# A graph layer on one core: gathers tied to the edge factors, tasks dealt anew, and four tensor operations moved from VectorE to GpSimd

## The chip, the core and the metric

The kernel runs on one core of a Trainium2 chip. The core has five engines with an instruction queue each: TensorE (PE, whose weight loads the profile lists apart as PEld), VectorE (DVE), ScalarE (ACT), GpSimd (POOL) and SyncE (SP), and 16 DMA engines. Each engine takes its instructions in the order in which the program gives them; between engines only semaphores order things. The metric is the device time of one execution in microseconds (us), lower is better.

## What is computed

A layer of a graph network with 1250 nodes of 512 features and 40000 edges, sorted by their target `dst`. Cut to what matters:

```python
# x: (1250, 512); per edge: source, target, a 3-vector n, a distance r
s_j   = silu(x[src][:, 384:] @ W1 + b1) @ W3 + b3            # a table of 1250 rows
basis = sqrt(2/R) * sin(k*pi*r/R) / r * cutoff(r) @ W2 + b2   # k = 1..20
s1, s2, s3 = split(s_j * basis)
msg = [ v_j * s1 + s3 * n ,  s2 ]                             # 384 + 128 features
x   = x + segment_sum(msg, dst)                               # first sum over edges
row = update(x)                                               # per node: U, V, Wu1, Wu2
x   = x + segment_sum(row[src], dst)                          # second sum over edges
out = layernorm(x_in + x)
```

## The kernel before

**Front.** A table with one row of 640 floats per node (128 + 128 factors and the scaled vector part) is computed in ten blocks and written to DRAM. Edge data are turned by TensorE so that edges lie on the partitions.

**Main loop.** The 40000 edges are cut into chunks of 512, four chunks to a group (20 groups). A step `t` takes tile `i` of each of the four chunks of group `g`: four tiles of 128 edges. `NT` is 80 steps, four per group, and the groups go in pairs, so that the work repeats every eight steps. In each step:

- `gather` (POOL, L693) issues four indirect DMAs that fetch the source rows into `rows_t`, of which there are four buffers, and then two memsets of a tile `idle` that nobody reads (L704). It is called two steps ahead (`ahead = 2`).
- `edge_factors` (PE, L792) multiplies the basis with `W2` into `eb`. There is one `eb` tile in PSUM: the factors of step t+1 can be written only when `messages(t)` has read those of step t.
- `messages` (DVE, L804 and L807) multiplies rows and factors. Between its two products `make_pair` (DVE, L821) marks target and source for the links.
- `add_messages` (PE, L838, L845) sums the messages of step t-1 into the window of their group, `count_links` (PE, L863) counts how often each source occurs for each target, and `mark_sources` (ACT, L777, L780) makes the one-hots for that.

**Per group.** `make_turns` (DVE L713, L719, L723; ACT L725 the sine) makes the sines' arguments for two groups at once, `make_basis` (DVE, L734) the basis of a group, `turn_basis` (PE L743, copied by ACT L748) transposes it for `edge_factors`; `make_hot` (L752) and `make_spread` (L765, two halves) on DVE make the matrices that PE sums with. `close_group` copies the sums out of PSUM and splits the counts on ACT; `add_counts` finishes them on DVE.

**Per block of 128 nodes (two groups).** A chain over some ten steps (`sum_block`, `take_block`, `turn_nodes`, `times_u`, `times_uv`, `lengths`, `root`, `hidden`, `curve`, `factors`, `scale_row`, `end_row`) computes the node's second message, which is split in three bf16 parts: `part_row` and `less_part` (ACT L1048, DVE L1050, L1053). `begin_out` already multiplies counts with finished parts for some of the output blocks in PSUM.

**End.** After the loop the last block's chain runs, `add_out` does the remaining products, POOL adds up the rests (L1103, L1105), and `end_out` and `norm_out` normalize and store.

**What sets the order.** Nothing is scheduled automatically. The steps' tasks are put in lists by hand (`first`, `early`, `late`, `dve`), and the loop runs these lists at fixed places of a step. The order on each engine is the order of these calls. The loop's core:

```python
        for t in range(max(*early, *late, *dve) + 1):
            if t + ahead < NT:
                gather(t + ahead)
            if t < NT:
                messages(t)
            run(first, t)
            ...
```

Of the kernel before, what the change touches and what calls it, by code (L numbers as in the profile page):

```python
# [20 lines left out]
P = 128  # L21
# [516 lines left out]
def windowed(tc, sh):  # L538
# [55 lines left out]
    resid = tc.dram_tile([NP, width], F32, name="resid")  # L594
    counts = sh.counts
# [10 lines left out]
    with tc.tile_pool(name="msg", bufs=4) as pool, tc.tile_pool(  # L606
# [15 lines left out]
        quarter = pool.tile([P, 1], F32, name="quarter", bufs=1)  # L622
        fade = pool.tile([P, NE], F32, name="fade", bufs=1)
# [8 lines left out]
        def ratios():  # L632
            nc.vector.tensor_scalar(ratio, every, 1.0 / R_CUT, 1.0, op0=ALU.mult, op1=ALU.min)
            nc.vector.memset(quarter, 0.25 * TWO_PI)

# [50 lines left out]
        idle = pool.tile([P, 2, 160], F32, name="idle", bufs=1)  # L686

        def gather(t):
            g, i = batches[t]
            rows_t = pool.tile([P, CPG, V + 2 * C], F32, name="rows_t", bufs=ROWS)  # L690
            for j in tiles(g, i):
                n = lanes(g, i, j)
                nc.gpsimd.indirect_dma_start(  # L693
                    out=rows_t[:n, j, :],
                    out_offset=None,
                    in_=sh.table1,
                    in_offset=bass.IndirectOffsetOnAxis(
                        ap=sh.src_i[:n, g, i * CPG + j : i * CPG + j + 1], axis=0
                    ),
                )  # L700
            rows_of[t] = rows_t

            for k in range(2):
                nc.gpsimd.memset(idle[:, k, :], 0.0)  # L704


        def make_turns(g, n, part):
# [3 lines left out]
            if part == 0:  # L711
                share = ratio[:, g * EPG : (g + n) * EPG].rearrange("p (g t) -> p g t", t=EPG)
                nc.vector.tensor_mul(  # L713
# [10 lines left out]
            if part == 3 or part == 2 and g > 0:  # L724
                nc.scalar.activation(args, args, AF.Sin, scale=TWO_PI)  # L725
# [7 lines left out]
        def make_basis(g):  # L733
            nc.vector.tensor_mul(  # L734
# [35 lines left out]

        def mark_sources(t):

            g, i = batches[t]
            one = pool.tile([P, CPG, P], F16, name="one", bufs=3)
            for j in tiles(g, i):
                e = g * EPG + i * CPG + j
                nc.scalar.activation(one[:, j, :], number[:, :P], AF.Abs, bias=low[:, e : e + 1])  # L777
            for j in tiles(g, i):
                e = g * EPG + i * CPG + j
                nc.scalar.activation(  # L780
                    one[:, j, :], one[:, j, :], AF.Relu,
                    scale=less[:, e : e + 1], bias=worth[:, e : e + 1],
                )
            onehots[t] = one


        def edge_factors(t):
            g, i = batches[t]
            eb = ps_work.tile([P, CPG, BANK], F32, name="eb")
            for j in tiles(g, i):  # L790
                rows = slice(j * FEAT, j * FEAT + N_RBF + 1)
                nc.tensor.matmul(  # L792
# [3 lines left out]
            ebs[t] = eb  # L796

        def messages(t):
# [6 lines left out]
            make_pair(t)  # L805
            for js, n, m in runs(g, i):
# [64 lines left out]
        def close_group(g):  # L871
# [5 lines left out]
            else:  # L877
                if g + 2 < NGR:
                    assert rows == P
                    sums[g + 2] = pool.tile([P, width], F32, name="sums_1", bufs=2)  # L880
                    nc.scalar.copy(sums[g + 2][P - WIN :, :], agg[P - WIN :, :])
# [3 lines left out]
                rows = min(rows, KEPT)  # L885
                nc.scalar.copy(sums[g][:rows, :], agg[:rows, :])
# [7 lines left out]
            boths[g] = both  # L894

        def add_counts(g):
            both = boths.pop(g)
# [3 lines left out]
            del adjs[g]  # L901

# [19 lines left out]
        def sum_block(b):  # L922
            blk = work()
            for k in range(2):
                nc.tensor.matmul(
                    blk, sh.sel[:, k, :], sums.pop(2 * b + k), start=(k == 0), stop=(k == 1)
                )
            blks[b] = blk
# [116 lines left out]
        def part_row(b, k):  # L1045
# [3 lines left out]
            else:  # L1049
                nc.vector.tensor_sub(table2(b, 2), x1s.pop(b), table2(b, 1))  # L1050

        def less_part(b):
            nc.vector.tensor_sub(x1s[b], x1s[b], table2(b, 0))  # L1053
# [27 lines left out]
        def load_x(first):  # L1081
# [5 lines left out]
            for b in range(first, first + n):  # L1087
                if b in (0, NB - 1):
                    load_nodes(nc.scalar, sh, to, b, b + 1, cols, first)
            inner = [b for b in range(first, first + n) if b not in (0, NB - 1)]  # L1090
            load_nodes(nc.scalar, sh, to, inner[0], inner[-1] + 1, cols, first)
            for k in range(n):
                kept[first + k] = to[:, k, :]

        def load_rest(first):
            n = min(5, NB - first)
            to = five_rows("msg", 2)
            nc.scalar.dma_start(to[:, :n, :], rows_from(resid, first, n))
# [20 lines left out]
        def begin_out(b, a, last, kept):  # L1119
            if a == 0:  # L1120
                accs[b] = ps_sum.tile([P, BANK], F32, name="begun")
            products(accs[b], b, a, a + 1, a == 0, last and not kept)
            if last and not kept:
                partial[b] = pool.tile([P, width], F32, name=f"begun_{b}", bufs=1)
                nc.scalar.copy(partial[b], accs.pop(b))
# [9 lines left out]
        def end_out(b):  # L1135
# [8 lines left out]
            nc.vector.tensor_scalar(scale[:, 0:1], moments[:, 1:2], EPS, None, op0=ALU.add)  # L1144
            nc.scalar.activation(scale[:, 0:1], scale[:, 0:1], AF.Sqrt)
            ending[b] = row, moments, scale

        def norm_out(b):
            row, moments, scale = ending.pop(b)
            nc.vector.reciprocal(scale[:, 0:1], scale[:, 0:1])  # L1150
            nc.vector.tensor_scalar(
                scale[:, 1:2], moments[:, 0:1], scale[:, 0:1], -1.0, op0=ALU.mult, op1=ALU.mult
            )
# [11 lines left out]
        first, early, late, dve = {}, {}, {}, {}  # L1165

        def at(when, step, fn, *args):
            when.setdefault(step, []).append((fn, args))

        def pair_turns(g, part, t):  # L1170
            n = min(2, NGR - g)
            if n > 0:
                at(dve, t, make_turns, g, n, part)

        for k in range(3):
            pair_turns(1, k, 0)
        for g in range(NGR):
            at(early, last_step[g] + 1, close_group, g)
            at(dve, last_step[g] + 1, add_counts, g)
        for t, (g, i) in enumerate(batches):  # L1180
            if t + 1 < NT:
                at(early, t, mark_sources, t + 1)
            if g + 1 < NGR:
                if g % 2:
                    if i == 0:
                        at(dve, t, make_hot, g + 1)
                        at(early, t, turn_basis, g + 1)
                    elif i == 1:
                        at(dve, t, make_spread, g + 1, 0)
                        pair_turns(g + 2, 0, t)  # L1190
                    elif i == 2:
                        at(dve, t, make_spread, g + 1, 1)
                else:
                    if i == 1:
                        at(dve, t, make_hot, g + 1)
                    elif i == 2:
                        at(dve, t, make_basis, g + 1)
                        at(dve, t, make_spread, g + 1, 0)
                    elif i == 3:
                        at(first, t, turn_basis, g + 1)  # L1200
                        at(dve, t, make_spread, g + 1, 1)
                        if g + 2 < NGR:
                            at(dve, t, make_basis, g + 2)
        begin, begins, ends = 0, [], {}
        for b in range(NB):
            begin = max(last_step[2 * b + 1] + 1, begin + 8)
            at(late, begin, sum_block, b)
            at(dve, begin + 1, take_block, b)
            at(dve, begin + 2, keep_rest, b)
            at(early, begin + 2, turn_nodes, b)  # L1210
            at(early, begin + 3, times_u, b)
            at(late, begin + 3, times_uv, b)
            at(late, begin + 4, lengths, b)
            at(first, begin + 5, root, b)
            at(early, begin + 5, hidden, b)
            at(first, begin + 6, curve, b)
            at(early, begin + 6, factors, b)
            at(dve, begin + 7, scale_row, b)
            at(first, begin + 8, end_row, b)
            begins.append(begin)  # L1220
            ends[b] = end = begin + 8
            steps = (1, 4, 5, 6) if end < NT else (0, 0, 0, 0)
            for when, step, fn, *args in (
                (first, steps[0], part_row, b, 0), (dve, steps[1], less_part, b),
                (late, steps[2], part_row, b, 1), (dve, steps[3], part_row, b, 2),
            ):
                at(when if end < NT else dve, end + step, fn, *args)

        for g in range(3, NGR, 2):
            pair_turns(g, 1, last_step[g - 2])  # L1230
            pair_turns(g, 2, last_step[g - 2] + 1)
# [3 lines left out]
        for c, of in zip(range(4, NB), ((1,), (3,), (0, 4), (5,), (6,), (2,))):  # L1235
            for k, b in enumerate(of):
                n = begun[b] = c - 1 if k == len(of) - 1 else c - 2
                begin, long = begins[c - 1] + 4 * k, 8 // len(of)
                for a in range(n):
                    t = begin + a * (long - 1) // (n - 1)  # L1240
                    at(early, t, begin_out, b, a, a == n - 1, c == NB - 1)
# [3 lines left out]
        for first_b in range(0, NB, 5):  # L1245
            at(dve, free, load_x, first_b)
# [454 lines left out]
```

## Time and profile before

| | |
|---|---|
| median of 17 runs | 555.43 us (551.39 to 559.36) |
| the profiled execution | 555.12 us; span in the profile 553.2 us, so 1.9 us lie around it |
| granted TensorE clock, mean | 0.921 |
| PE | 445.0 us busy, 80% |
| DVE | 431.8 us busy, 78% |
| ACT | 359.2 us busy, 65% |
| POOL | 392.1 us busy, 71% |
| the gathers' DMA queue (q0) | 104.86 MB, 63.5% of 16 engines |
| first gather starts, last gather ends | 34.99 us, 473.65 us |
| last message of the loop ends | 489.85 us |

A row of the groups gives line, engine, operation, output and inputs, the count, the busy time and the mean of one in ns, and the idle time of the engine just before with what ended it ("issue": nothing that the profile shows). A row of the timeline gives start, length, engine, line and operation.

### The profile page before, as it was taken

To read this page: it belongs to the slowest core of one execution; us is meant where nothing else is said; L and a number is where in the kernel's file an instruction comes from. 1 tells how busy PE (TensorE), PEld (TensorE's weight loads), DVE (VectorE), ACT (ScalarE), POOL (GpSimd) and SP (SyncE) were. 2 spreads that over 40 slices of the span, in tenths; PEclk is the share of its full clock that TensorE was granted. 3 is DMA by queue.
4 is the path that set the end of the run, shared out by engine and by line. 5 is a ranking of instruction groups with operands and counts; after the bars stand their busy time and mean duration, and the time that the engine had idled before them with its cause. 6 is when DMAs were issued, how large, how long until landed. Compare 5 with 4: busy or idle time off the path is not lost.

```text
span 553.2 us, 11300 instructions
## 1 busy us (share of the span) xinstructions
PE 445.0 (80%) x4318; PEld 236.8 (43%) x4318; DVE 431.8 (78%) x594; ACT 359.2 (65%) x897; POOL 392.1 (71%) x524
## 2 busy tenths in 40 slices
PE   3945667678878878887887888989798788999993
PEld 2522323344444444444444445445444444445441
DVE  6587877978798898697999889789789789551682
ACT  1436473774887779379588687867957958723341
POOL 7338888887888788787888888888888888200960
PEclk9965888968898998797999999899899899999998
DMA  8557888878888877787788788778878778309131
GB/s 250 203 172 222 235 234 238 266 230 239 253 249 233 242 241 228 238 263 229 231 257 241 227 253 250 230 232 256 243 233 258 228 238 239 91 0 329 66 133 61
DMA packets 35179, 121.19 MB, mean 219 GB/s; under 512 B 6365, under 2 KB 7912, under 8 KB 35116
## 3 DMA queue, kind: packets, MB, share of 16 engines
q0 software_dynamic: 26016, 104.86, 63.5%
q1 hardware_dynamic: 5124, 9.69, 4.8%
q10 hardware_dynamic: 3976, 5.82, 3.1%
q8 instruction: 36, 0.59, 0.4%
q14 instruction: 27, 0.22, 0.1%
HBM read 111.89 MB, written 8.46 MB: 218 GB/s over the span
## 4 chain that ended last, share of the span: by engine, by line
PE 35%; DVE 23%; POOL 16%; ACT 9%; issue 8%; DMA 8%; DVEq 0%; POOLq 0%; ACTq 0%
POOL rows_t L693 13%; DVE msg L807 10%; PE agg L838 6%; PE eb L792 5%; DVE msg L804 5%; PE agg L845 5%; DMA wu_sb<-in_L_gnn_Wu_dram 4%; PE work L986 4%; DVE pair L821 3%; DMA rows_t<-table,src_i 3%; PE adj L1110 2%; PE agg L1110 2%; PE eb L1110 2%; ACT one L780 2%; PE begun L1110 2%
## 5 line engine op out<-in xcount | busy, mean ns | idle before, releaser
L693 POOL DMA_INDIRECT rows_t<-table,src_i x313 | 321.0, 1025 | 97.9 <-issue 81.2
L807 DVE TENSOR_TENSOR msg<-rows_t,eb 128x1536 f32<-128x1536 f32 (+1 forms) x81 | 137.0, 1692 | 0.0
L780 ACT ACTIVATE one<-one,weight,src_f 128x128 f16<-128x128 f16 x313 | 128.2, 481 | 0.2 <-DVE magic L674 0.2
L804 DVE TENSOR_TENSOR msg<-rows_t,eb 128x1024 f32<-128x1024 f32 (+1 forms) x81 | 95.4, 1178 | 40.5 <-PE eb L792 30.7
L792 PE MATMUL eb<-w_sb,basis_t 21*128 21x384 f32 x626 | 77.5, 551 | 61.2 <-DVE msg L807 60.2
L777 ACT ACTIVATE one<-number,low 128x128 f16<-128x128 f16 x313 | 99.4, 389 | 2.9 <-PE adj L863 1.5
L838 PE MATMUL agg<-msg,hot 128*32 128x512 f32 x626 | 97.9, 683 | 0.0
L845 PEld LDWEIGHTS agg<-msg,spread 128*32 128x32 f32 x1878 | 63.0, 122 | 59.3 <-issue 58.8
L845 PE MATMUL agg<-msg,spread 128*32 128x128 f32 x1878 | 77.1, 298 | 0.0
L792 PEld LDWEIGHTS eb<-w_sb,basis_t 21*128 21x128 f32 x626 | 27.2, 188 | 86.0 <-issue 58.4
L1110 PEld LDWEIGHTS <-counts 128*128 128x128 f16 x300 | 29.1, 98 | 27.6 <-issue 2.4
L1103 POOL TENSOR_TENSOR msg<-msg,rows_t 128x512 f32<-128x512 f32 (+1 forms) x10 | 13.9, 1399 | 37.2 <-PE eb L1110 37.2
L898 DVE SCALAR_TENSOR_TENSOR both<-both,adj 128x400 f16<-128x400 f16 (+1 forms) x20 | 11.3, 567 | 35.8 <-ACT both L893 29.2
L821 DVE TENSOR_TENSOR pair<-number,column 128x640 f16<-128x640 f16 (+1 forms) x81 | 38.2, 473 | 0.0
L863 PE MATMUL adj<-pair,one 128*128 128x160 f16 x313 | 38.2, 248 | 0.0
L765 DVE TENSOR_TENSOR spread<-hot,attr 128x768 f32<-128x768 f32 x40 | 37.9, 950 | 0.0
L704 POOL MEMSET idle<- 128x160 f32 x160 | 34.5, 254 | 0.0
L986 PE MATMUL work<-ident,square 128*128 128x128 f32 x60 | 14.0, 381 | 22.7 <-ACT basis_t L748 22.7
L1110 PE MATMUL begun<-store,counts 128*128 128x512 bf16 x117 | 31.5, 379 | 0.0
L1043 ACT COPY x<-work 128x128 f32<-128x128 f32 x10 | 2.7, 265 | 42.0 <-PE work L986 42.0
L863 PEld LDWEIGHTS <-one 128*128 128x128 f16 x313 | 21.3, 102 | 18.0 <-issue 15.4
L838 PEld LDWEIGHTS agg<-msg,hot 128*32 128x32 f32 x626 | 13.2, 112 | 34.0 <-issue 24.6
(171 smaller groups left out, 577.3 us busy)
## 6 DMA issues: line engine op xcount, KB each, us to landing
rows_t<-table,src_i POOLq DMA_INDIRECT x313
resid<-x SPq DMA_DIRECT2D x10, 256.0 KB
msg<-resid ACTq DMA_DIRECT2D x2, 1280.0 KB
rows_t<-in_x_dram ACTq DMA_DIRECT2D x2, 1024.0 KB
out_dram<-msg SPq DMA_DIRECT2D x8, 256.0 KB
table<-msg SPq DMA_DIRECT2D x6, 320.0 KB
store<-in_x_dram POOLq DMA_DIRECT2D x2, 768.0 KB
table<-rows_t SPq DMA_DIRECT2D x4, 320.0 KB
```

Of the source, the lines that this page charges most:

```text
L693: nc.gpsimd.indirect_dma_start(out=rows_t[:n, j, :], out_offset=None, in_=sh.table1, in_offset=bass.IndirectOffsetOnAxis(ap=sh.src_i[:n, g ...
L765: nc.vector.tensor_mul(spread[g][:, at], hots[g][:, at, None, :].to_broadcast([P, n, 3, WIN]), sh.attr[:, g, at, :, None].to_broadcast([P, ...
L777: nc.scalar.activation(one[:, j, :], number[:, :P], AF.Abs, bias=low[:, e : e + 1])
L780: nc.scalar.activation(one[:, j, :], one[:, j, :], AF.Relu, scale=less[:, e : e + 1], bias=worth[:, e : e + 1],)
L792: nc.tensor.matmul(eb[:, j, :V], turned[g][rows, i, :], sh.w2_sb[rows, :], start=True, stop=True,)
L804: nc.vector.tensor_mul(msg[:m, js, V:], rows_t[:m, js, V:], eb[:m, js, C:V])
L807: nc.vector.tensor_mul(msg[:m, js, :V].rearrange("p t (k c) -> p t k c", k=3), rows_t[:m, js, :V].rearrange("p t (k c) -> p t k c", k=3), ...
L821: nc.vector.tensor_tensor(pair[:m, js, :].rearrange("p t (l h) -> p t l h", h=2), number[:m, : PARTS * WIN].rearrange("p (l h) -> p l h", ...
L838: nc.tensor.matmul(agg[j * WIN : (j + 1) * WIN, :], hots[g][:m, i * CPG + j, :], msg[:m, j, :width], start=(i == 0), stop=False, skip_grou ...
L845: nc.tensor.matmul(agg[j * WIN : (j + 1) * WIN, c * C : (c + 1) * C], spread[g][:m, i * CPG + j, c, :], msg[:m, j, width:], start=False, s ...
L863: nc.tensor.matmul(to[:, :, at : at + WIN], one[:m, j, :], pair[:m, j, :].rearrange("e (p n) -> e p n", n=WIN), start=(i == 0 and j == js[ ...
L1110: nc.tensor.matmul(acc, counts[:, a, b * P : (b + 1) * P], table2(a, k), start=(start and a == first and k == 0), stop=(stop and a == end ...
```

## The change

Gathers: the two memsets go; a gather is called three steps ahead instead of two, after `edge_factors(t + 1)`, and its first DMA waits for the last matmul of these factors. Four operations move from DVE to POOL: `make_basis` (but for group 0), the product of `make_turns` (but for the first groups), and for all blocks but the last the two subtractions `less_part` and the third `part_row`; they stand in a new list `pool_` that runs right after the gather of a step. `make_pair` comes after both products of `messages`. The tasks of a group and of a block are dealt to other steps and carry a rank within a step; `close_group` copies the rows that the next odd group needs last, and `add_counts` is split in two. In the front all table rows come before the turning of weights and vectors. Other output blocks are begun in the loop (0 to 7, 120 matmuls instead of 111 there), each is stored to DRAM and loaded at the end, and the end's loads are issued by SP instead of ACT. In `end_out` and `norm_out` two small DVE operations become ACT operations.

```diff
-        def gather(t):
+        def gather(t, behind=None):
             ...
-                nc.gpsimd.indirect_dma_start(
+                got = nc.gpsimd.indirect_dma_start(
             ...
+                if behind is not None and j == 0:
+                    tc.add_manual_dep(
+                        got.ins, behind.ins.name, sync,
+                        reason="so that rows come while PE is ahead of DVE",
+                    )
             rows_of[t] = rows_t
-
-            for k in range(2):
-                nc.gpsimd.memset(idle[:, k, :], 0.0)
...
             if part == 0:
+                engine = nc.gpsimd if g > 1 else nc.vector
                 ...
-                nc.vector.tensor_mul(
+                engine.tensor_mul(
...
-        def make_basis(g):
-            nc.vector.tensor_mul(
+        def make_basis(g, engine):
+            engine.tensor_mul(
...
                 nc.vector.tensor_mul(msg[:m, js, V:], rows_t[:m, js, V:], eb[:m, js, C:V])
-            make_pair(t)
-            for js, n, m in runs(g, i):
...
-                nc.vector.tensor_sub(table2(b, 2), x1s.pop(b), table2(b, 1))
+                engine = nc.gpsimd if b < NB - 1 else nc.vector
+                engine.tensor_sub(table2(b, 2), x1s.pop(b), table2(b, 1))
 
         def less_part(b):
-            nc.vector.tensor_sub(x1s[b], x1s[b], table2(b, 0))
+            engine = nc.gpsimd if b < NB - 1 else nc.vector
+            engine.tensor_sub(x1s[b], x1s[b], table2(b, 0))
...
+        for g in range(1, NGR, 2):
+            base, n = 4 * g - 4, min(2, NGR - g)
+            at(pool_ if g > 1 else dve, max(0, base - 2), 4, make_turns, g, n, 0)
+            at(dve, max(0, base - 1), 6, make_turns, g, n, 1)
+            at(dve, base, 6, make_turns, g, n, 2)
+            at(dve, base, 6, make_turns, g, n, 3)
+            at(dve, base + 2, 4, make_hot, g)
+            at(pool_, base + 2, 5, make_basis, g, nc.gpsimd)
+            at(first, base + 3, 1, turn_basis, g)
+            at(dve, base + 3, 2, make_spread, g, 0)
+            at(dve, base + 4, 2, make_spread, g, 1)
+            if n > 1:
+                at(pool_, base + 4, 4, make_basis, g + 1, nc.gpsimd)
+                at(early, base + 5, 1, turn_basis, g + 1)
+                ...
...
-        ahead = 2
+        ahead = 3
...
-        for t in range(max(*early, *late, *dve) + 1):
-            if t + ahead < NT:
-                gather(t + ahead)
+        for t in range(max(*first, *early, *late, *dve, *pool_) + 1):
             if t < NT:
                 messages(t)
+            if t < NT:
+                make_pair(t)
+            ...
             run(first, t)
             if 1 <= t <= NT:
                 add_messages(t - 1)
                 count_links(t - 1)
             run(early, t)
             if t + 1 < NT:
-                edge_factors(t + 1)
+                made = edge_factors(t + 1)
+            if t + ahead < NT:
+                gather(t + ahead, made)
+            run(pool_, t)
             run(late, t)
             run(dve, t)
```

## The prediction

> **What bounds the kernel now.** I read the waits of POOL first, then the groups of POOL and DVE, then the timeline of POOL inside the loop, then that of PE.
>
> The waits (engine and line, what ended the wait, us in total, times, longest):
>
> ```profile
> POOL rows_t L693 <- issue: 81.2, 296, 0.3
> ...
> POOL rows_t L693 <- DVE spread L765: 1.5, 9, 0.2
> ...
> POOL rows_t L693 <- DVE msg L807: 1.0, 5, 0.4
> ```
>
> The gathers hardly ever wait for a buffer or for data (under 3 us); their idle time is the pause that POOL takes between two of its own instructions. The groups give its size:
>
> ```profile
> L693 POOL DMA_INDIRECT rows_t<-table,src_i x313 | 321.0, 1025 | 97.9 <-issue 81.2 <-DVE fade L644 14.0 <-DVE spread L765 1.5
> L704 POOL MEMSET idle<- 128x160 f32 x160 | 34.5, 254 | 0.0
> L734 DVE TENSOR_TENSOR basis<-turn,fade 128x320 f32<-128x320 f32 x20 | 13.7, 686 | 0.1
> L713 DVE TENSOR_TENSOR turn<-ratio,half_n 128x640 f32<-128x640 f32 (+1 forms) x11 | 8.3, 757 | 0.0
> L1053 DVE TENSOR_TENSOR x<-x,store 128x512 f32<-128x512 f32 x10 | 6.8, 682 | 2.4 <-ACT store L1048 2.4
> L1103 POOL TENSOR_TENSOR msg<-msg,rows_t 128x512 f32<-128x512 f32 (+1 forms) x10 | 13.9, 1399 | 37.2 <-PE eb L1110 37.2
> ```
>
> Gathers 321.0, pauses 97.9 - 14.0 (the wait before the first) = 83.9, memsets 34.5: 439.4 us, and the stretch from the first gather (34.99) to the end of the last (473.65) is 438.7. POOL is one unbroken chain over the whole loop. Eight steps take 44.7 us (the fixed pattern returns at 252.29, 297.00 and 341.49). DVE is nearly as full: about 39 busy us in each such stretch by the windows, and it ends 16.2 us after the last gather, though rows need only 3.0 to 3.4 us from a gather's end to their message (51.91 to 54.91, 57.35 to 60.72). So POOL sets the pace and DVE falls slowly behind it.
>
> The timeline of POOL, one step (a pair of memsets of 0.42 ends just before it):
>
> ```profile
> 331.63 0.96 POOL L693 DMA_INDIRECT rows_t<-table,src_i  x1 [0.16 <-issue]
> 332.90 0.95 POOL L693 DMA_INDIRECT rows_t<-table,src_i  x1 [0.30 <-issue]
> 334.15 0.95 POOL L693 DMA_INDIRECT rows_t<-table,src_i  x1 [0.30 <-issue]
> 335.40 0.95 POOL L693 DMA_INDIRECT rows_t<-table,src_i  x1 [0.30 <-issue]
> 336.34 0.43 POOL L704 MEMSET idle<- 128x160 f32 x2
> ```
>
> A gather after a gather starts 0.30 late, one after a memset 0.16, and a memset starts when the gather before it ends. Two memsets thus cost 0.42 + 0.16 - 0.30 = 0.28 us a step.
>
> The timeline of PE, after it stood still for 3.14 us, and then in full run:
>
> ```profile
> 255.52 1.65 PE L986 MATMUL work<-ident,square 128*128 128x128 f32 x6 [3.14 <-ACT basis_t L748]
> 257.10 1.94 PE L838 MATMUL agg<-msg,hot 128*32 128x512 f32 x8
> 260.25 0.72 PE L863 MATMUL adj<-pair,one 128*128 128x160 f16 x4
> 260.75 0.64 PE L1003 MATMUL work<-n_t,wu_sb 128*128 128x128 f32 x2
> 261.55 0.93 PE L792 MATMUL eb<-w_sb,basis_t 21*128 21x384 f32 x8
> ...
> 332.18 0.66 PE L743 MATMUL work<-ident,basis 128*128 128x128 f32 x4
> 332.77 1.06 PE L838 MATMUL agg<-msg,hot 128*32 128x512 f32 x8
> 334.42 0.45 PE L863 MATMUL adj<-pair,one 128*128 128x160 f16 x4
> ```
>
> After such a pause PE works at half speed for some 5 us: sums and links of a step take 3.15 + 0.50 us instead of 1.65 + 0.30.
>
> **The change, part by part.** All sums are made against the profiled 555.1 us (0.3 below the median).
>
> *POOL's own work.* The memsets go: -34.5. Added until the last gather: 19 bases, 8 products of 640 elements and one of 320, 14 subtractions of 512. POOL's only row of this kind is L1103: 1.27 us for 512 elements at its undisturbed median. A basis on DVE takes 0.686 us, where 320 plain elements take 0.49 (L645), so the strides cost 1.4 times; 1.27 x 320/512 x 1.4 = 1.1, without strides 0.79, and I take 1.0. 19 x 1.0 + 8 x 1.58 + 0.79 + 14 x 1.27 = 50.2. For each basis the bounds are 0.69 (DVE's) and 1.5 (a disturbed POOL row of 1.75 scaled), -6 and +10 in all. Pauses: 270 x 0.30 + 42 x 0.16 = 87.7. With 321.0 for gathers, less 3 because DVE has some 10% fewer two-operand operations that lengthen a gather (0.949 median, 1.025 mean), POOL's chain is 455.9 without any wait.
>
> The Trainium skill, "GPSIMD Engine Reference", section "Engine selection", speaks against this move: two-input elementwise work belongs on VectorE, GpSimd being about 2 times slower; by that factor the 50.2 would be an estimated 60.
>
> *The new wait.* This decides. `gather(t+3)` waits for `edge_factors(t+1)`, and the tensor work of `pool_` stands behind that gather. In step base+2 of each eight, POOL gathers four times and only then makes the basis of group g. PE's next task but for begun products is `turn_basis(g)`, first of step base+3. Behind it in PE's queue are sums and links of a step, `turn_nodes`, and `edge_factors(base+4)`. The next gather on POOL waits for just these factors. So from the end of the basis POOL stands still until PE has done all that. DVE has already caught up and waits as well, and nothing else covers it. PE has by then stood still for over 5 us (it waited for four gathers and a basis), so I take the slow rows: hand-over 0.15 (basis to transpose at 35.87 to 36.02), transposes 1.1 (L743 at 36.02), 3.15 sums, 0.50 links, 0.45 `turn_nodes`, 0.93 factors, hand-over 0.15: 6.4 us. In full run it is 0.15 + 0.6 + 1.65 + 0.3 + 0.45 + 0.93 + 0.15 = 4.2.
>
> The second basis of a pair is made in step base+4 behind `gather(base+7)`; `turn_basis(g+1)` stands in step base+5 after sums and links, right before `edge_factors(base+6)`, for which POOL's next gather waits: 0.15 + 1.1 + 1.66 (slow factors, 47.16) + 0.15 = 3.1, in full run 1.8.
>
> There are ten first and nine second bases: 10 x 6.4 + 9 x 3.1 = 92, less the 19 pauses of 0.16 that this contains: 89. In full run 58 - 3 = 55. The other six gathers of eight steps find their factors done: those of step t+1 are there 3.3 (rows) + 2.9 (messages) + 0.9 = 7.1 us after the end of `gather(t)`, and POOL comes to `gather(t+3)` two sets of gathers, 10 us or more, after that end. The least is left just after the second basis, where PE comes late: about even.
>
> The skill's same page, section "Instruction dispatch", says that a Pool instruction does not hold back the next one until it is complete; if tensor work began up to a gather's length (0.95) early, an estimated 40 us would come off. The memsets, which start at the gather's end every time, show none of it.
>
> *DVE, ACT, PE in the loop.* DVE loses 3.6 us in eight steps (two bases, a product of 0.82, two subtractions), `messages` free the factors 0.41 sooner, and `close_group` hands its counts over sooner: the waits for these (L898 29.2, L804 for `eb` 30.7) may go. Against a slower POOL all that is slack, so 0. If POOL were no bound, it would be 4 to 10 us in eight steps.
>
> *Front.* Table rows follow each other every 1.2 us where nothing lies between and every 1.5 where something does; the first gather comes 1.4 earlier. *After the last gather.* DVE no longer lags: 3.3 for the rows and 2.2 for the messages instead of 16.2, -10.7. The end loses 24 products of 0.216 us on PE's last chain (-5.2), but 5 more blocks of sums (15 products, 3.2 us) lie beside the last block's chain, which is a step shorter: -4, between -8 and +4. The stores and loads of begun blocks lie on SP behind few other transfers; POOL's two additional sums at the end (2.6) lie under PE's products.
>
> *Sum.* 555.1 + (455.9 - 439.4) + 89 - 1.4 - 10.7 - 4 = 644.5; I say 643.
>
> **Rivals.**
> 1. *The same waits with PE at full speed.* For it: idle time before the slow rows above may not be the only cause. Against it: the pauses of 3.14 us (255.52) and 2.79 us (300.23) are both followed by slow rows. 34 us less: 610.
> 2. *Dearer*: disturbed gathers and tensor operations, or the even wait after the second basis costing 1 to 3 us each: above 672.
> 3. *No waits*: PE reaches `turn_basis` only after the basis is there. Then 643 - 89 = 554: no change or a little slower. It would need PE some 5 us later in each step than DVE's messages let it be.
> 4. *Faster*: tensor work on POOL runs beside the gathers' descriptor work and costs nothing, so that bases come before PE asks. POOL's chain is 318 + 312 x 0.30 = 412, DVE's eight steps 44.7 - 3.6, about equal: 412 - 439 - 1.4 - 10.7 - 4, or 511. It decides once a basis ends within 1 us of the factors that its gather waits for; the order of POOL's rows (a memset never begins before the gather's end) speaks against it.
>
> **How the numbers follow.** Forecast 0.62, rival 1 0.22, rival 2 0.06, rival 3 0.05, rival 4 0.05. From 600 (rival 1 with cheap bases) to 672 (forecast with bases at 1.5 and gathers slowed by 0.06) lie about 0.82. A measurement of this kernel can tell 0.3% (1.7 us) from no change. Slower: 0.62 + 0.22 + 0.06 + 0.02 of rival 3; same 0.02; faster 0.05 + 0.01.
>
> **What would show it.** POOL: no L704, gathers still about 1.0 us, tensor rows of 1.0 to 1.6 us, and before one gather in eight steps a wait of about 6 us released by PE's `eb`, before another one of 3. PE: waits of 5 us or more before L750 released by POOL's basis, then slow sums. DVE near 65% busy, its waits on rows or `eb`. Eight steps of about 56 us. Eight steps under 45 us, or gathers that never wait for PE, would make me wrong.

## The result, and the profile after

The change makes the kernel slower: 685.85 us median against 555.11 (47 runs), a ratio of 1.236 with a 95% interval of 1.232 to 1.239. The prediction said 643 (600 to 672): the direction and most of the mechanism were right, the size was 43 us short. The profiled execution took 686.44 us, its span 684.5 us. Two later pairs of runs, marked below, ran where every kernel was slower, the kernel before included (688 and 704 us), and are read by their ratios alone.

The waits of the kernel after (engine and line, what ended the wait, us in total, times, longest):

```profile
DVE msg L817 <- PE eb L804: 174.2, 47, 9.7
...
PE work L750 <- POOL basis L741: 97.3, 19, 7.6
POOL rows_t L697 <- PE eb L804: 84.2, 27, 7.0
POOL rows_t L697 <- issue: 76.5, 255, 0.3
...
POOL rows_t L697 <- PE begun L1132: 36.5, 12, 7.2
...
PE begun L1132 <- POOL store L1064: 26.6, 5, 5.9
```

The gathers, which had next to no waits before, now wait for PE; PE waits for POOL; VectorE waits for PE. No engine is full: PE 72%, POOL 58%, VectorE 59% of the span. The last row is small, but the prediction has nothing of it: PE waits five times for POOL's third part of a row (L1064).

The groups of POOL in the kernel after give the price of its new work:

```profile
L741 POOL TENSOR_TENSOR basis<-turn,fade 128x320 f32<-128x320 f32 x19 | 16.9, 889 | 0.3
...
L720 POOL TENSOR_TENSOR turn<-ratio,half_n 128x640 f32<-128x640 f32 (+1 forms) x9 | 11.0, 1221 | 0.2
...
L1064 POOL TENSOR_TENSOR store<-x,store 128x512 bf16<-128x512 f32 x9 | 10.5, 1165 | 1.1 <-ACT store L1061 1.0
```

The second row mixes two shapes; its eight products of 640 elements take 1.28 us each. All three kinds are 8 to 19% cheaper than estimated (1.0, 1.58 and 1.27 us), so POOL's own work is not where the missing time is.

The timeline of the kernel after, around a first basis and the gather behind it:

```profile
351.22 0.89 POOL L741 TENSOR_TENSOR basis<-turn,fade 128x320 f32<-128x320 f32 x1
...
352.17 1.12 PE L750 MATMUL work<-ident,basis 128*128 128x128 f32 x4 [5.30 <-POOL basis L741]
...
353.21 1.94 PE L849 MATMUL agg<-msg,hot 128*32 128x512 f32 x8
...
356.92 0.93 PE L804 MATMUL eb<-w_sb,basis_t 21*128 21x384 f32 x8
...
358.23 0.99 POOL L697 DMA_INDIRECT rows_t<-table,src_i  x1 [6.11 <-PE begun L1132]
```

This is the predicted ring. The basis ends at 352.11, PE does transposes, sums at half speed (1.94 us; 1.06 in full run), links, `turn_nodes` and the factors, and POOL starts again 6.11 us later. PE itself had stood still for 5.30. (A label names what ended last by the profile: "PE begun" on the gather's wait is the product that stands behind the factors on PE. All 35 first gathers of a step with a pause over 0.45 us start 0.29 to 0.39 us after the last of their factors.) Sorted by the step that issues the gather, POOL's pauses over 0.45 us are 58.9 us in nine first-basis steps and 6.9 in the tenth (6.6 each; predicted 6.4), and 24.2 us in nine second-basis steps (2.7 each; predicted 3.1).

The same timeline 23 us earlier shows the wait that the prediction lacks:

```profile
326.87 1.15 POOL L697 DMA_INDIRECT rows_t<-table,src_i  x1 [0.30 <-issue]
...
328.05 1.16 POOL L1064 TENSOR_TENSOR store<-x,store 128x512 bf16<-128x512 f32 x1
329.26 0.59 PE L1132 MATMUL begun<-store,counts 128*128 128x512 bf16 x1 [5.38 <-POOL store L1064]
...
334.84 1.12 PE L804 MATMUL eb<-w_sb,basis_t 21*128 21x384 f32 x8
...
336.28 0.96 POOL L697 DMA_INDIRECT rows_t<-table,src_i  x1 [7.07 <-DVE turn L730]
```

`part_row(b, 2)` is the fourth of POOL's moved operations, dealt to step `end + 5` = 8b + 23, behind that step's four gathers. For blocks 2 to 6, the last begun product that needs this row stands in the slot `(7, late)` of the same step. PE must wait for POOL's subtraction (5.38 us), and the factors that POOL's next gather waits for stand behind that product. The label "DVE turn" on the gather's wait names an operation that happened to end at 336.26 and whose result the gather does not read; the factors ended at 335.96, and the gather starts 0.32 us after that, like the others. Five such steps cost 33.7 us, 6.7 each.

Busy time by stretch of the kernel after, from about the end of one second basis to the next, so eight steps each (us, then busy times of PE, PEld, DVE, ACT, POOL with instruction counts, then TensorE's granted clock, the DMA share and GB/s):

```profile
193.66:249.68 56.02, 37.79 (x402) 20.21 (x402) 36.18 (x42) 33.94 (x86) 36.96 (x38) 0.86 0.64 193
249.68:307.02 57.34, 41.14 (x405) 21.73 (x405) 36.19 (x42) 34.28 (x86) 36.87 (x37) 0.79 0.62 188
307.02:368.90 61.88, 44.43 (x420) 22.28 (x420) 35.94 (x42) 35.21 (x88) 36.98 (x37) 0.81 0.60 183
```

Up to 307 a cycle takes about the predicted 56 us (56.0 and 57.3), after it 62, although POOL and VectorE do the same work in all three: the third wait sets in with the first begun product that needs a row of the same step.

### The profile page after: what moved, and what is told of

It reads as the page before. It is cut to its first block, busy times and chain, and to the rows that moved or that the text cites. A ratio compares the mean times of both kernels' runs of the same rounds, so it can differ in the third digit from the quotient of the medians.

```text
span 684.5 us, 11239 instructions
## 1 busy us (share of the span) xinstructions
PE 489.6 (72%) x4318; PEld 248.4 (36%) x4318; DVE 407.3 (59%) x529; ACT 367.3 (54%) x919; POOL 397.6 (58%) x412
## 4 chain that ended last, share of the span: by engine, by line
POOL 37%; PE 29%; issue 20%; DMA 6%; DVE 4%; ACT 4%; POOLq 0%; DVEq 0%; ACTq 0%
POOL rows_t L697 31%; PE agg L849 5%; PE agg L856 4%; PE eb L804 3%; PE begun L1132 3%; DMA bu_sb<-in_L_gnn_bu_dram 3%; POOL basis L741 2%; PE work L939 2%; DVE msg L817 2%; PE adj L874 2%; PE adj L1132 2%; DVE msg L818 1%; PE work L999 1%; PE eb L1132 1%; DMA rows_t<-table,src_i 1%
## 5 line engine op out<-in xcount | busy, mean ns | idle before, releaser
L697 POOL DMA_INDIRECT rows_t<-table,src_i x313 | 309.4, 989 | 234.3 <-PE eb L804 84.2
L849 PE MATMUL agg<-msg,hot 128*32 128x512 f32 x626 | 108.9, 757 | 0.0
L804 PE MATMUL eb<-w_sb,basis_t 21*128 21x384 f32 x626 | 84.3, 599 | 26.1 <-DVE msg L818 25.3
L750 PE MATMUL work<-ident,basis 128*128 128x128 f32 x80 | 20.4, 404 | 99.2 <-POOL basis L741 97.3
L856 PE MATMUL agg<-msg,spread 128*32 128x128 f32 x1878 | 81.6, 310 | 0.0
L755 ACT COPY basis_t<-work 128x512 f32<-128x512 f32 x20 | 11.7, 586 | 128.6 <-PE work L750 128.6
L1132 PE MATMUL begun<-store,counts 128*128 128x512 bf16 x138 | 44.1, 428 | 26.6 <-POOL store L1064 26.6
L750 PEld LDWEIGHTS work<-ident,basis 128*128 128x128 f32 x80 | 12.9, 199 | 107.3 <-POOL basis L741 105.1
L772 DVE TENSOR_TENSOR spread<-hot,attr 128x768 f32<-128x768 f32 x40 | 43.9, 1099 | 0.0
L1061 ACT CAST store<-x 128x512 bf16<-128x512 f32 x20 | 12.4, 620 | 41.0 <-POOL x L1068 39.7
L909 DVE SCALAR_TENSOR_TENSOR both<-both,adj 128x400 f16<-128x400 f16 (+1 forms) x20 | 11.2, 562 | 27.2 <-ACT both L900 27.2
```

The source lines that it names most:

```text
L697: got = nc.gpsimd.indirect_dma_start(out=rows_t[:n, j, :], out_offset=None, in_=sh.table1, in_offset=bass.IndirectOffsetOnAxis(ap=sh.src_i ...
L772: nc.vector.tensor_mul(spread[g][:, at], hots[g][:, at, None, :].to_broadcast([P, n, 3, WIN]), sh.attr[:, g, at, :, None].to_broadcast([P, ...
L804: made = nc.tensor.matmul(eb[:, j, :V], turned[g][rows, i, :], sh.w2_sb[rows, :], start=True, stop=True,)
L849: nc.tensor.matmul(agg[j * WIN : (j + 1) * WIN, :], hots[g][:m, i * CPG + j, :], msg[:m, j, :width], start=(i == 0), stop=False, skip_grou ...
L856: nc.tensor.matmul(agg[j * WIN : (j + 1) * WIN, c * C : (c + 1) * C], spread[g][:m, i * CPG + j, c, :], msg[:m, j, width:], start=False, s ...
L1132: nc.tensor.matmul(acc, counts[:, a, b * P : (b + 1) * P], table2(a, k), start=(start and a == first and k == 0), stop=(stop and a == end ...
```

## Experiments

Each edit is against the change unless the text says otherwise.

**1. The third part on VectorE.**

```diff
-                engine = nc.gpsimd if b < NB - 1 else nc.vector
-                engine.tensor_sub(table2(b, 2), x1s.pop(b), table2(b, 1))
+                nc.vector.tensor_sub(table2(b, 2), x1s.pop(b), table2(b, 1))
...
-                parts = ..., (pool_, end + 5, 3)
+                parts = ..., (early, end + 5, 9)
```

> The change, but the rows' third part of all blocks is subtracted by VectorE, in the same step, ahead of the factors. Theory (a third stall that the prediction missed: in each of the last five cycles the last begun product on PE waits for the third part, which stands on POOL behind four gathers of the same step, and the factors for the next gather stand behind that product on PE): the pauses of 6.7 us, five times, go (-33.7), and nine POOL subtractions of 1.17 with their pause of 0.16 go (-12) where POOL then sets the pace: 640 to 652 us. Rival (only POOL's load counts, the stall merely moves to another link): -12 or less, 674 to 686.

Measured: 651.58 us (650.71 to 652.47), 34.3 less than the change. PE's waits before the begun products for POOL are gone from the list, and no pause over 0.45 us is left in the steps where the 33.7 us were; the bases' pauses are what they were (57.7 and 24.7 us). The third wait is shown; its size is shown less exactly, since the edit also takes work from POOL. Of the 34.0 us by which the stretch of the gathers gets shorter, 5.1 are POOL's own work, and its pauses over 0.45 us fall by 29.4 in sum: the 33.7 are gone, some 4 came back at other places. With this wait and this work removed, 651.6 lies within the predicted range.

**2. The bases on VectorE.**

```diff
-            at(pool_, base + 2, 5, make_basis, g, nc.gpsimd)
+            at(dve, base + 2, 5, make_basis, g, nc.vector)
...
-                at(pool_, base + 4, 4, make_basis, g + 1, nc.gpsimd)
+                at(dve, base + 4, 4, make_basis, g + 1, nc.vector)
```

> The change, but all bases are multiplied by VectorE, in the same steps and at the end of its list. Theory (ring of waits: a basis stands on POOL behind four gathers, PE's transposes wait for it, the factors stand behind the transposes, the next gather waits for the factors): the 19 pauses that the trace shows at these places go (58.9 + 6.9 + 24.2 = 90), and 19 bases of 0.89 with 0.16 of pause go (-20): 576 to 600 us; the pauses of 6.7 us at the third parts are still there. Rival (VectorE becomes the bound or PE waits for VectorE's basis as long): above 620.

Measured: 597.73 us (595.48 to 599.64), 88 less. The bases' pauses are gone; five pauses of 6.1 us in the steps of the third part remain (30.6 us), as expected, and eight of 2.0 us have come up in the step ahead of them. The time fell although VectorE had 19 bases more to do.

**3. The same work, ahead of the gather.**

```diff
             if t + 1 < NT:
                 made = edge_factors(t + 1)
+            run(pool_, t)
             if t + ahead < NT:
                 gather(t + ahead, made)
-            run(pool_, t)
```

> The change, but in each step POOL's tensor work is issued before the gather instead of behind it; nothing else is moved, and POOL does all that it did. Theory (what costs is the place behind a gather that waits for factors, not POOL's work): all three kinds of pauses go, 90 + 33.7, and the time is 555 to 575 us. Rival 1 (POOL's work itself is what costs): 660 to 690. Rival 2 (the bases' ring is opened, the third part is still late): 590 to 600.

Measured: 571.72 us (570.33 to 572.38), 114 less by moving one line. The stretch from the first gather to the end of the last is 459.3 us; the prediction's sum for POOL without any wait was 455.9. The waits of this kernel:

```profile
PE begun L1132 <- POOL store L1064: 21.7, 5, 4.6
PE work L750 <- POOL basis L741: 17.8, 9, 4.0
POOL rows_t L697 <- PE eb L804: 15.0, 14, 2.1
```

PE still waits five times for the third part, but POOL hardly waits in turn: of its five pauses of 6.7 us in these steps, four of 1.1 to 1.5 are left. The waits left are those of a slower chain for the faster one, not a ring. So it was the place behind a gather that waits, and not POOL's tensor work, that cost most of the loss.

**4. No wait of the gather for factors.**

```diff
-                gather(t + ahead, made)
+                gather(t + ahead)
```

> The change, but a gather does not wait for factors; it waits for its buffer of rows alone, which the messages of four steps before set free. POOL's tensor work stays behind the gather. Theory (the ring is closed by the factors' wait): POOL runs a step further ahead, the bases are there before PE asks, and POOL's chain without waits, 33 + 440 + 75, gives 550 to 575 us. Rival (the ring closes over the buffers just as well, since PE still asks for the basis before it makes the factors that VectorE's messages need): 640 to 690.

Measured: 570.02 us (568.82 to 572.38). The ring opens here too, with all tensor work in its old place. Experiments 3 and 4 agree within 0.3%: each leaves POOL's chain nearly unbroken, 459.3 and 454.6 us from the first gather to the end of the last, of which 16.3 and 5.9 are pauses over 0.45 us.

**5. Order mended, bases on VectorE** (edits 2 and 3 together).

> POOL's tensor work ahead of the gather of its step, and the bases on VectorE; products and subtractions stay on POOL. Theory (with the order mended POOL's chain of 459 us sets the time, so what is taken from it comes off until VectorE is full): 19 x (0.89 + 0.16) = 20 us less than with the bases on POOL, 550 to 556 us, about the kernel before. Rival (VectorE is full already): 562 to 572, as with the bases on POOL.

Measured: 552.64 us (550.79 to 554.74), 19 less than experiment 3; ratio to the kernel before 0.994 (0.991 to 0.998). With the ring open, what is taken from POOL comes off almost in full: of the expected 20 us, 16.2 in the stretch of the gathers (459.3 to 443.1; the gathers themselves got 3.6 longer in sum) and some 2 at the front and the end.

**6. No tensor work on POOL** (edits 1 and 2, and likewise these two).

```diff
-            engine = nc.gpsimd if b < NB - 1 else nc.vector
-            engine.tensor_sub(x1s[b], x1s[b], table2(b, 0))
+            nc.vector.tensor_sub(x1s[b], x1s[b], table2(b, 0))
...
-            at(pool_ if g > 1 else dve, max(0, base - 2), 4, make_turns, g, n, 0)
+            at(dve, max(0, base - 2), 4, make_turns, g, n, 0)
```

> The change without any tensor work on POOL: bases, the product of the sines' arguments, both subtractions of the rows go back to VectorE; gathers still wait for factors and tasks are dealt as in the change. POOL alone would need 312 x (0.99 + 0.30) = 403 us for its gathers. Theory (with POOL free VectorE is the bound: the change's 400 busy us of VectorE up to the last message, plus 19 bases of 0.69, 9 products of about 0.8 and 18 subtractions of 0.68, are 433, at the 93% that it reaches in the kernel before 465; then 63.5 us to the end, 33 at the front, of which VectorE's 400 hold some 15): 540 to 560, no better than before. Rival (POOL's gathers still set the pace): 33 + 403 + 5 + 63.5, or 500 to 520.

Measured: 528.43 us (526.1 to 531.4), ratio to the kernel before 0.948 (0.941 to 0.956): faster than both kernels, and between the two expectations. The windows of this kernel, first over the stretch of the gathers to the last message (columns as above), show who is full:

```profile
33.56:465.93 432.37, 365.35 (x3950) 191.73 (x3980) 378.56 (x470) 330.04 (x834) 321.17 (x314) 0.93 0.82 254
```

VectorE is busy for 378.6 of 432.4 us, not 420: the expectation added up durations of instructions that overlap each other a little (added up, they are 410 here). POOL's gathers set the pace: up to the last of them 320.5 us of gathers and 312 pauses of 0.30 are 414 of the 420.8 us. The rival was right on the bound and too low in its terms: gathers of 1.02 instead of 0.99, and 11.6 us from the last gather to the last message instead of 5.

**7. The kernel before, without its idle memsets.**

```diff
             rows_of[t] = rows_t
-
-            for k in range(2):
-                nc.gpsimd.memset(idle[:, k, :], 0.0)
```

> The kernel before without its 160 idle memsets on POOL. The prediction's reading (POOL sets the pace; two memsets cost a step 0.28 us): POOL's chain gets 22 us shorter, 530 to 538 us if VectorE could follow. Second theory (VectorE is as full: it ends 16.2 us after the last gather where 5 would do, busy 424 of the 455 us up to there): POOL runs ahead and VectorE does not, 548 to 556, and the lag of VectorE's last message grows from 16 to over 25 us or the gathers wait for buffers.

Measured: 549.81 us (547.84 to 552.11), ratio to the kernel before 0.989 (0.982 to 0.997). Of the 22 us that POOL's chain could have lost, 8 came off (438.7 to 430.9): gathers got 5 us longer in sum and wait 11.9 us for buffers that VectorE frees, where they had waited 1.0. So POOL and VectorE were both nearly the bound before, and part of the time VectorE took over. The lag of VectorE did not grow (16.4 us); the buffers stop the gathers first. Against this kernel, experiment 6 has 21 us less with as few operations on POOL. One visible part: VectorE's wait for ScalarE's `both` fell from 31.0 to 1.3 us. That is what the rest of the change is worth, the new dealing, the third step ahead, the front and the end together; which of its moves does it was not taken apart.

**8. The last products behind the last chain** (on top of experiment 3).

```diff
-        for n, (b, a) in enumerate(units):
-            when, step = spare[n * len(spare) // len(units)]
-            at(when, step, 7, add_out, b, a, a + 1)
+        for b, a in units:
+            at(late, ends[NB - 1], 7, add_out, b, a, a + 1)
```

> POOL's tensor work ahead of the gather (as in the run of that name), and the 31 units of output products that stand beside the last block's chain are all put behind it. Theory (in the change the chain from the last block's sum to its row's last part is held up by PE, which makes these products in between: 27.2 us instead of 22.5 in the kernel before): the chain takes 18 to 21 us, the 31 units of some 0.65 us follow it, and the time is 8 to 14 us longer than with the order alone, 578 to 586. Rival (the chain is long because of VectorE's and POOL's own work at the end): the chain stays at 26 to 28 and the time grows by the full 20 us, 590 or more.

Measured: 581.94 us (579.8 to 582.95), 10 more. The chain from the last block's sums to `end_row` falls from 27.2 to 20.7 us. So in the change it is PE's products between the links that lengthen the last chain, and not the work of POOL and VectorE at the end.

**9. Is the factors' wait itself worth something?** Experiment 6 without it (edit 4 on top), timed beside experiment 6 repeated.

> The same kernel as all_on_vector, timed again beside the next one on one chip: 523 to 533 us if it holds.

> As all_on_vector (no tensor work on POOL, tasks dealt as in the change), and gathers do not wait for factors either; what is left of the change is the new dealing. Theory (with nothing behind the gathers the wait for factors closes no ring; VectorE is full, 420 busy of 432 us, and POOL has slack): the same within 1%, 523 to 534 us, with VectorE's lag behind the last gather up from 11.6 to 15 us or more. Rival (the wait is what makes it fast, because without it gathers and VectorE's two-operand work meet more often): 540 to 550, as the kernel before without its memsets, which has no such wait either.

Measured: 606.7 us (606.24 to 608.72) with the wait, 703.9 (696.12 to 706.69) without, where the kernel before took 688.06: ratios 0.892 (0.886 to 0.898) and 1.031 (1.020 to 1.042). That fits neither expectation. The same pair once more:

> The kernel of all_on_vector once more. Where the kernel before takes some 555 us: 523 to 533. Where it takes some 688, as beside all_on_vector_again: 600 to 612.

> The kernel of all_vector_no_wait once more, to see whether its 704 us come from the missing wait or from where it ran (the kernel before took 688 us there, not 555). If they come from the place: 520 to 535 us where the kernel before takes 555, the same as with the wait within 1%. If the wait itself is what makes it fast: 540 us or more there.

Measured: 620.46 and 719.66 us beside 703.86 for the kernel before: ratios 0.888 (0.881 to 0.895) and 1.030 (1.020 to 1.040), the same again; both pairs are classed as unclear. Then the kernel without the wait alone:

> The kernel of all_vector_no_wait a third time, for a place where the kernel before takes its usual 555 us. If the factors' wait by itself costs and gains nothing there: 522 to 534 us, as all_on_vector. If it gains there too: 540 us or more, towards the 550 of the kernel before without memsets. Where the kernel before takes 688 or more again: 700 to 725.

Measured: 527.0 us (525.17 to 529.22) where the kernel before took 558.44, ratio 0.948 (0.940 to 0.955). Where the kernel before takes its 555 us, the wait costs nothing and gains nothing, once no work stands behind it: 527.0 against 528.4, the same ratio of 0.948. Where the kernel before took 688 and 704 us, the kernel with the wait took 14% less than the one without. Why is open: in the first trace without the wait, gathers wait 189.3 us for buffers that VectorE frees, and VectorE's messages wait 115.3 us for something that the profile does not name.

## Why the prediction was right or wrong

The prediction's sum was 644.5 us for an execution that took 686.4. Its parts against the trace:

| part | predicted | measured |
|---|---|---|
| POOL busy, first to last gather | 318 + 50.2 = 368.2 | 353.7 |
| short pauses | 87.7 | 83.2 |
| longer waits of gathers | 89 | 139.5 |
| sum of this stretch | 544.9 | 576.4 |
| last gather to the end | 64.9 | 75.1 |
| first gather at | 33.6 | 33.1 |

*The two basis waits: right.* Their place, their releasers, PE's slow sums behind them and their sizes (6.6 and 2.7 us for 6.4 and 3.1) are in the trace, and experiments 2, 3 and 4 take them away in three ways, experiment 3 but for 7.5 us. (The hand-over from the factors to the gather, taken as 0.15, was 0.3 to 0.4.) Rival 1 (PE at full speed) is wrong: the sums behind each of the ten first bases took 1.93 or 1.94 us. Rival 4 is wrong: the tensor rows start at the end of the gather before them (326.87 + 1.15, then 328.05). The 40 us that the prediction estimated from the Trainium skill, "GPSIMD Engine Reference", section "Instruction dispatch", did not come off either: none of the 43 tensor operations behind a gather starts before that gather's end. Rival 3, no waits, is what experiments 3 and 4 made (570 to 572 us; its 554 had the same wrong terms for the end).

*"The other six gathers of eight steps find their factors done": the step that failed.* The prediction followed POOL's bases from queue to queue and checked the remaining steps with an average (factors after 7.1 us, gathers after 10). It did not ask the same question of the third part: who on PE reads it, in which slot, and what stands behind that reader. The readers are the begun products, and their slots are in the kernel. It cost 33.7 us in five steps, where the prediction has 0; experiment 1, which takes it out, gave back 34.3, part of it POOL's work. Some 16 us more went into pauses of 0.6 to 2.7 us in the other steps and in the last, short groups.

*POOL's own work: over by 14.5.* Bases 0.889 us, products 1.28 for the long form, subtractions 1.165; gathers 0.989 for 1.016. The factor of 2 of the Trainium skill, "GPSIMD Engine Reference", section "Engine selection", with its estimated 60 us, was farther off: up to the last gather the tensor rows sum to 44.2 us, where the prediction took 50.2. These errors offset part of the missed wait.

*"After the last gather, −10.7": wrong.* The prediction counted rows and messages, 5.5 us. But a gather that waits for the factors of step t+1 brings the rows of step t+3, so behind the last gather two more sets of factors are still to be made. The timeline of the kernel after:

```profile
608.51 0.94 POOL L697 DMA_INDIRECT rows_t<-table,src_i  x1 [0.30 <-issue]
...
613.23 0.91 PE L804 MATMUL eb<-w_sb,basis_t 21*128 21x384 f32 x4
...
614.22 0.69 DVE L817 TENSOR_TENSOR msg<-rows_t,eb 128x512 f32<-128x512 f32 x1 [3.39 <-PE eb L804]
...
619.48 0.69 DVE L817 TENSOR_TENSOR msg<-rows_t,eb 128x512 f32<-128x512 f32 x1 [3.48 <-PE eb L804]
```

PE needs 5.3 us from one set to the next, and the last message ends 11.6 us after the last gather. The wait moved from VectorE's lag to PE.

*"The end, −4": nothing.* From the last message to the end it is 63.5 us, 63.4 before. PE's products at the very end became fewer, as counted, but those put beside the last chain made it 27.2 us long instead of 22.5 (experiment 8). The prediction took +3.2 for their own time and nothing for the links that they delay.

*The ranges.* The time came out above 672, where rival 2 stood with a chance of 0.06, but hardly for its reasons: gathers and tensor operations were cheaper, not dearer, and the wait that it feared just after the second basis came four times, 4.3 us in all.

## What to carry to other kernels

When work is moved to another queue, list for every moved operation, not only for the costliest, who reads its result and in which slot of that engine's queue, and whether anything behind that reader frees the queue it was moved to; such a ring costs the whole round trip each time, here 2.7 to 6.7 us for operations of about 1 us. An instruction that waits is a bad place to put work behind: the same work ahead of the waiting gather was 114 us faster, by one moved line. Before moving work off a full engine, see whether the receiving one is full too: here POOL needs 414 us for its gathers alone, and the best version gives it no other work.

## What was unexpected of the hardware

A tensor operation of POOL delays some of VectorE's and leaves others alone. The timeline of experiment 5:

```profile
160.33 1.75 DVE L818 TENSOR_TENSOR msg<-rows_t,eb 128x1536 f32<-128x1536 f32 x1
160.49 1.17 POOL L1068 TENSOR_TENSOR x<-x,store 128x512 f32<-128x512 f32 x1
...
161.99 0.48 DVE L832 TENSOR_TENSOR pair<-number,column 128x640 f16<-128x640 f16 x1
...
166.56 1.28 POOL L720 TENSOR_TENSOR turn<-ratio,half_n 128x640 f32<-128x640 f32 x1
166.59 1.60 DVE L832 TENSOR_TENSOR pair<-number,column 128x640 f16<-128x640 f16 x1
```

`pair`, both of whose inputs are in SBUF, takes 0.48 us alone and 1.60 beside a POOL operation of 1.28: about the overlap is added. `msg`, which has one input in PSUM, takes 1.75 us with or without. POOL's operation keeps its length here. In experiment 3 this made the `pair` group 58.1 us instead of the 38.3 of experiment 6, so part of what is taken from VectorE comes back as waiting. The Trainium skill, "SBUF — State Buffer", section "SBUF: two separate sides", says that a GpSimd operation and a VectorE one with two SBUF inputs exclude each other for a whole instruction, the first to start going on; `pair` at 166.59 agrees, as it started 0.03 us after POOL. A `spread` of the changed kernel does not, by the starts that the profile records:

```profile
451.62 2.44 DVE L772 TENSOR_TENSOR spread<-hot,attr 128x768 f32<-128x768 f32 x1
452.08 1.16 POOL L1064 TENSOR_TENSOR store<-x,store 128x512 bf16<-128x512 f32 x1
```

It started 0.46 us before POOL and still took 2.44 us instead of 0.95, while POOL kept its 1.16. Three more of these spreads (at 390.00, 513.35 and 574.09) did the same, and all four ended 0.83 us after POOL's operation, as if they had done hardly anything before it. Each had started while the gather ahead of that operation was still running. Where no gather stands ahead, one row at the end of experiment 1 agrees with the skill: VectorE's L1063 starts at 620.88, POOL's L1126 at 621.40, and it is POOL's that gets longer, 1.60 us instead of 1.27. By these rows a tensor operation that stands behind a gather goes on before a VectorE operation that started up to 0.46 us earlier; why is not shown.
